# Banded attention: row sums taken from the exponentials and weights divided on GpSimd, in place of products with ones and a division at the end

## The chip, the cores and the metric

The kernel runs on one core of a Trainium2 chip. A core has five engines with queues of their own: TensorE (PE in the profile, with its weight loads as PEld), VectorE (DVE), ScalarE (ACT), GpSimd (POOL) and SyncE (SP, which here only issues DMAs). Each executes its instructions in the order in which they were put into its queue, and they wait for one another by semaphores.

The metric is the device time of one launch in microseconds. A run's time is a little longer than the span that its profile shows. Times are compared as medians over runs.

## The reference, cut to what matters

The reference is two transformer layers on an input of 16 sequences of 256 positions and 128 features, in float32. Layer 0 is full attention (16 heads of 64) and a feed-forward stage that picks one of 64 small networks for each position; layer 1 is a gated mix of linear and windowed attention, and then causal attention with eight experts behind it. Only the windowed attention of layer 1 is touched here:

```python
# WINDOW = 64, HALF = 32, NWIN = 65, N_HEADS = 16, HEAD_DIM = 8
def score_step(_, w):
    off = w - HALF
    ks = jax.lax.dynamic_slice_in_dim(kp, w, S, axis=2)
    s = jnp.einsum('bhsd,bhsd->bhs', qh, ks) * scale
    s = s + rel_bias[off + WINDOW][None, :, None]
    valid = (pos + off >= 0) & (pos + off < S)
    s = jnp.where(valid[None, None, :], s, -jnp.inf)
    return (None, s)
_, scores = jax.lax.scan(score_step, None, jnp.arange(NWIN))
attn = jax.nn.softmax(scores, axis=0)

def out_step(acc, aw):
    a, w = aw
    vs = jax.lax.dynamic_slice_in_dim(vp, w, S, axis=2)
    return (acc + a[..., None] * vs, None)
```

Each position looks at the 65 positions from 32 before to 32 behind it. The softmax is over these 65 scores, for each of 16 heads of 8 features.

## The kernel before

The 16 sequences are worked as 8 groups of 512 positions (two sequences each). A group passes through five stages: A (layer 0's attention), B (its feed-forward), C (layer 1's gated attention), D (causal attention) and E (the experts). Functions `stage_a` to `stage_e` do not issue instructions. They add tasks to a plan (`W.add`), each with the engine or the choice of engines ("VS" is DVE or ACT), a cost in ns, the tiles that it reads and writes, and a due time `at`: group g's stage A is due at g, B at g+1, and so on to E at g+4, so that up to five groups are in flight. `Plan.order` then walks through the tasks as a list scheduler. At each step it takes the task that can begin first by the costs, and of equals the one due first; it picks the engine where there is a choice and gives each buffer a slot from the pool of its class. The order that comes out is written into the engines' queues as it stands. A change of one cost, one task or one pool size (`SLOTS`) therefore gives another order for everything behind it.

Pools that the change touches: `x` (the groups' activations, 512 floats in each partition), `xT` (stage A's transposed input), `k1` (small tiles of stages B, C and E), `c` (the tiles of stage C), `pbC` (weights of the banded attention). `NX` is the number of groups whose input is loaded at the start; x of a later group is loaded by L291, into the slot of a group that was written out (L1331).

The banded attention stands in `stage_c`, from L1011. Each of a group's two sequences is cut into four blocks of 64 queries, 64 blocks in all. A block's keys are `nk` positions, 96 at the ends of the sequence and 128 inside. Two heads share the partitions of a tile: 64 queries of one and 64 of the next, so 16 heads make eight columns `u` of width nk.

1. GpSimd spreads the queries over the heads (`masked`, L1020), and DVE writes the values into one of three `vm` tiles so that head 4j+l stands in strip j with zeros beside it (L1036).
2. PE multiplies queries and keys (`scores`, L1046).
3. DVE adds the band of biases with -1e30 outside (L1053) and takes the negated maximum of each column (L1054).
4. For each of two halves, ACT takes four exponentials (L1065), PE transposes them (L1071), and DVE or ACT moves the result to SBUF (`ptC`; L520 is the helper's ACT form, L522 its DVE form).
5. PE multiplies with the values (`values`, L1078): for `what` 0 with `vm`, and for `what` 1 with `hones`, a tile of ones in the same strips. The second run of 16 products gives each query's sum of exponentials, repeated over the head's eight features.
6. DVE takes the reciprocal of the sums (L1098) and multiplies (L1099) into `winT`, which the gate at L1110 reads.

`mm` at L514 is the helper of every matrix product, so L514 stands for all of them in the profile; the tiles tell them apart. Stages A and D share the function `pair`: there ACT sums its exponentials as it takes them (L623, `accum_out`), DVE takes the reciprocals (L630), GpSimd divides (L636), and PE transposes (L651).

Of the kernel before, what the change touches and what calls it, by code (L numbers as in the profile page):

```python
# [30 lines left out]
NFC = FF // P  # L31
NEG = -1.0e30
EPS = 1e-5
NX = 6
NBURST = 2

OFF = {"a": 0.0, "b": 1.0, "c": 2.0, "d": 3.0, "e": 4.0}

SLOTS = (
    ("x", 512, 6),  # L40
    ("xT", 512, 2),
    ("ua", 512, 6),
    ("ud", 512, 6),
    ("pb", 512, 4),
    ("pt", 512, 4),
    ("ov", 256, 8),
    ("m", 64, 26),
    ("k1", 256, 5),
    ("b", 512, 2),
    ("sc", 288, 1),  # L50
    ("c", 512, 9),
    ("qm", 512, 2),
    ("pbC", 512, 2),
    ("ptC", 512, 2),
    ("d", 512, 3),
    ("h2", 512, 2),
# [181 lines left out]
def kernel(ctx: ExitStack, tc: tile.TileContext, a: dict, out: bass.AP):  # L238
# [8 lines left out]
    def ctile(name, shape, dtype=F32):  # L247
        return const.tile(shape, dtype, name=name, tag=name)
# [223 lines left out]
    nc.gpsimd.affine_select(  # L472
        out=hm, in_=hm, compare_op=ALU.is_ge, fill=0.0, base=WD - 1, pattern=[[WD, WH]], channel_multiplier=-1
    )

    hones = ctile("hones", [P, 4, 4 * WD])
    nc.gpsimd.memset(hones, 0.0)
    for l in range(4):
        nc.gpsimd.memset(hones[:, l, l * WD : (l + 1) * WD], 1.0)

    NVM = 3
    vms = []
# [30 lines left out]
    def mm(o, lhsT, rhs, start=True, stop=True):  # L513
        nc.tensor.matmul(o, lhsT=lhsT, rhs=rhs, start=start, stop=stop)  # L514
# [409 lines left out]
    def stage_c(g):  # L924
# [48 lines left out]
        for b in range(2):  # L973
            W.at = base + 0.1 + 0.4 * b

            pkv, kv = W.buf("p", "pkv"), W.buf("k1", "kv")

            def outer(b=b, pkv=pkv):
                for i in range(2):
                    k = kl(J, d=D)[:, 2 * b + i, :]  # L980
                    mm(pkv()[:, :D], k, vl(J, d=D)[:, 2 * b + i, :], start=i == 0, stop=i == 1)
                for i in range(2):
                    k = kl(J, d=D)[:, 2 * b + i, :]
                    mm(pkv()[:, D : D + 1], k, ones1, start=i == 0, stop=i == 1)

            W.add("P", pe(P, count=4), outer, r=[kl, vl], w=[pkv], hold=[kv])
            W.add("VS", (dve(129), scl(129)), lambda e, pkv=pkv, kv=kv: copy(e, kv()[:, : D + 1], pkv()[:, : D + 1]), r=[pkv], w=[kv])
            pn, rden = W.buf("p", "pn"), W.buf("m", "rden")

            def numer(b=b, pn=pn, kv=kv):  # L990
                for i in range(2):
                    j = 2 * b + i
                    mm(pn()[:, i * 256 : i * 256 + D + 1], ql()[:, j * P : (j + 1) * P], kv()[:, : D + 1])

            W.add("P", pe(P + 1, count=2), numer, r=[ql, kv], w=[pn], hold=[rden, lin])
            pn2 = lambda pn=pn: pn("p (i n) -> p i n", i=2)

            def divide(b=b, pn2=pn2, rden=rden):
                r = rden()[:, :2]
                V.tensor_scalar(r, pn2()[:, :, D], 1e-6, None, ALU.add)  # L1000
                V.reciprocal(r, r)
                V.tensor_tensor(
                    out=lin(J, d=D)[:, 2 * b : 2 * b + 2, :], in0=pn2()[:, :, :D],
                    in1=r.unsqueeze(2).to_broadcast([P, 2, D]), op=ALU.mult,
                )

            W.add("V", 360 + dve(256), divide, r=[pn], w=[rden, (lin, b)])

            for i, (w0, w1_) in enumerate(win_of):  # L1011
                W.at = base + 0.1 + 0.4 * b + 0.09 * i
                nk = w1_ - w0
                t0 = w0 - (QC * i - HALF)
                c0 = b * S + QC * i
                qm = W.buf("qm", "qm")
                nq = [P, WH // 2, QC]

                def masked(e, qm=qm, c0=c0, nq=nq):
                    (V if e == "V" else G).tensor_tensor(  # L1020
                        out=qm("p (h q) -> p h q", q=QC), in0=qw()[:, c0 : c0 + QC].unsqueeze(1).to_broadcast(nq),
                        in1=hm8.unsqueeze(2).to_broadcast(nq), op=ALU.mult,
                    )

                W.add("G", (gps(512),), lambda masked=masked: masked("G"), r=[qw], w=[qm])

                iv = nblock[0] % NVM
                nblock[0] += 1
                vm, vt = vms[iv], vmt[iv]
                pvw = W.buf("p", "pvw")  # L1030
                W.add("P", pe(P), lambda pvw=pvw, w0=w0, w1_=w1_, nk=nk, b=b: mm(pvw()[:nk, :D], hT()[:, b * S + w0 : b * S + w1_], wvw), r=[hT], w=[pvw, vt])

                def spread(pvw=pvw, vm=vm, nk=nk):
                    for l in range(4):
                        own = lambda t: t.rearrange("p (g e) -> p g e", e=4 * WD)[:, :, l * WD : (l + 1) * WD]
                        V.tensor_tensor(out=own(vm[:nk, l, :]), in0=own(pvw()[:nk, :D]), in1=own(bvw[:nk, :]), op=ALU.add)  # L1036

                W.add("V", 4 * dve(32), spread, r=[pvw], w=[vt])
                sps = W.buf("s", "spsC")

                def scores(sps=sps, qm=qm, w0=w0, w1_=w1_, nk=nk, b=b):
                    s4 = sps("p (t u k) -> p t u k", t=2, u=4)
                    for u in range(4):
                        for t in range(2):
                            r = slice(t * 64, (t + 1) * 64)
                            mm(s4[:, t, u, :nk], qm()[r, u * P : (u + 1) * P], kw()[r, b * S + w0 : b * S + w1_])  # L1046

                W.add("P", pe(nk, count=4), scores, r=[qm, kw], w=[sps, chain_c[0]], mode="r")
                nmx = W.buf("m", "nmxC")

                def top(sps=sps, nmx=nmx, nk=nk, t0=t0):
                    s8 = sps("p (u k) -> p u k", u=8)[:, :, :nk]
                    V.tensor_tensor(out=s8, in0=s8, in1=band[:, :, t0 : t0 + nk], op=ALU.add)  # L1053
                    V.tensor_reduce(nmx()[:, :8], s8, AX.X, ALU.max, negate=True)  # L1054

                W.add("V", 130 + 2 * dve(8 * nk), top, w=[sps, nmx])
                pts = []
                for half in range(2):
                    pb, pt, tps = W.buf("pbC", "pbC"), W.buf("ptC", "ptC"), W.buf("p", "tpsC")

                    def weigh(sps=sps, nmx=nmx, pb=pb, half=half, nk=nk):
                        s8 = sps("p (u k) -> p u k", u=8)
                        for u in range(4):
                            hp = 4 * half + u
                            act(pb("p (u k) -> p u k", u=4)[:, u, :nk], s8[:, hp, :nk], AF.Exp, bias=nmx()[:, hp : hp + 1])  # L1065

                    W.add("S", 4 * (146 + 0.81 * nk), weigh, r=[sps, nmx], w=[pb], table="exp")

                    def turn(pb=pb, tps=tps, nk=nk):
                        for u in range(4):  # L1070
                            nc.tensor.transpose(tps("p (u k) -> p u k", u=4)[:nk, u, :], pb("p (u k) -> p u k", u=4)[:, u, :nk], ident)  # L1071

                    W.add("P", pe(P, count=4, passes=1), turn, r=[pb], w=[tps, chain_c[1]], hold=[pt])
                    W.add("VS", (dve(512), scl(512)), lambda e, pt=pt, tps=tps, nk=nk: copy(e, pt()[:nk, :], tps()[:nk, :]), r=[tps], w=[pt])
                    pts.append(pt)
                po = W.buf("p", "poC")

                def values(po=po, pts=pts, vm=vm, nk=nk):  # L1078

                    for what in range(2):  # L1080
                        for l in range(4):
                            for j in range(4):
                                r = slice(32 * j, 32 * j + 32)
                                h = 4 * j + l
                                c = ((h // 2) % 4) * P + (h % 2) * QC
                                mm(
                                    po()[r, what * QC : (what + 1) * QC],
                                    hones[:nk, l, :] if what else vm[:nk, l, r],
                                    pts[j // 2]()[:nk, c : c + QC],
                                    start=l == 0,  # L1090
                                    stop=l == 3,
                                )

                W.add("P", 1200, values, r=[vt] + pts, w=[po, chain_c[2]], hold=[winT], mode="c32")
                rw = W.buf("m", "rw")

                def divide(po=po, rw=rw, c0=c0):
                    V.reciprocal(rw()[:, :QC], po()[:, QC : 2 * QC])  # L1098
                    V.tensor_tensor(out=winT()[:, c0 : c0 + QC], in0=po()[:, :QC], in1=rw()[:, :QC], op=ALU.mult)  # L1099

                W.add("V", 700, divide, r=[po], w=[rw, (winT, (b, i))])

        W.at = base + 0.95
        linT = W.buf("c", "linT")
# [273 lines left out]
```

## Time and profile before

| | |
|---|---|
| median of three runs | 2264.16 us (2259.54 to 2265.47) |
| time of the profiled run | 2259.16 us |
| its span in the profile | 2257.3 us, mean granted PE clock 0.98 |
| exponentials of the banded attention, L1065 | 512 |
| its transposes, L1071 | 512 |
| products with `vm`, records on PE | 2048, 43.2 us busy |
| DMA | 47.98 MB, 21 GB/s over the span |

A line of the groups of instructions reads: line, engine, operation, written tile <- read tiles, shapes, count | busy time in us, mean ns of one | idle time of the engine just before them, and what ended most of it. A float32 matrix product shows as two records. Tiles are named by their pool: `p` and `s` are PSUM, `m` holds small columns. A line of the list of waits reads: who waited, for whom, then us in sum, times, and the longest.

In the slices, a digit is the busy share of a fortieth of the span in tenths. Ends of matmuls are modelled, so the busy time of PE is a little more than what it holds the engine; the start of the next record is the safer mark. Spans on POOL are rough.

### The profile page before, as it was taken

To read this page: it belongs to the slowest core of one execution; us is meant where nothing else is said; L and a number is where in the kernel's file an instruction comes from. 1 tells how busy PE (TensorE), PEld (TensorE's weight loads), DVE (VectorE), ACT (ScalarE), POOL (GpSimd) and SP (SyncE) were. 2 spreads that over 40 slices of the span, in tenths; PEclk is the share of its full clock that TensorE was granted. 3 is DMA by queue.
4 is the path that set the end of the run, shared out by engine and by line. 5 is a ranking of instruction groups with operands and counts; after the bars stand their busy time and mean duration, and the time that the engine had idled before them with its cause. 6 is when DMAs were issued, how large, how long until landed. Compare 5 with 4: busy or idle time off the path is not lost.

```text
span 2257.3 us, 50085 instructions
## 1 busy us (share of the span) xinstructions
PE 2126.6 (94%) x18474; PEld 1611.8 (71%) x18474; DVE 1711.4 (76%) x5167; ACT 1316.0 (58%) x3824; POOL 801.7 (36%) x1441
## 2 busy tenths in 40 slices
PE   6999999999999999999999999999899989989987
PEld 5777767777777677776777767777667767767755
DVE  4789898888678977688767897588876976785741
ACT  3556656666466656565565666565565645654642
POOL 6435352444143531335213352143521441330421
PEclk8999999999999999999999999999999999999998
DMA  6100000000100001100010000100011001001101
GB/s 149 24 1 2 2 1 1 2 2 20 43 16 11 2 15 38 34 1 2 15 47 20 2 1 25 48 11 2 1 38 39 7 19 37 22 7 51 29 20 42
DMA packets 61029, 47.98 MB, mean 21 GB/s; under 512 B 4609, under 2 KB 51297, under 8 KB 60785
## 3 DMA queue, kind: packets, MB, share of 16 engines
q1 hardware_dynamic: 59200, 43.09, 6.8%
q8 instruction: 146, 2.39, 0.5%
q0 software_dynamic: 1008, 0.65, 0.3%
q10 hardware_dynamic: 576, 1.05, 0.2%
q14 instruction: 99, 0.80, 0.1%
HBM read 41.89 MB, written 2.88 MB: 20 GB/s over the span
## 4 chain that ended last, share of the span: by engine, by line
PE 31%; DVE 16%; ACT 3%; issue 2%; POOL 1%; POOLq 0%; DVEq 0%; ACTq 0%
PE p L514 25%; PE p L651 2%; PE s L514 2%; DVE m L602 2%; DVE s L597 1%; ACT pb L623 1%; DVE m L606 1%; DVE m L531 1%; POOL pb L636 1%; DVE s L1053 1%; DVE m L1054 1%; PE p L1071 1%; DVE m L1147 1%; DVE pt L522 1%; DVE m L1149 1%
## 5 line engine op out<-in xcount | busy, mean ns | idle before, releaser
L636 POOL TENSOR_SCALAR pb<-pb,m 128x256 f32<-128x256 f32 (+1 forms) x1024 | 452.4, 458 | 710.6 <-DVE m L630 611.2
L1309 ACT ACTIVATE hid<-p,b 128x512 f32<-128x512 f32 x256 | 169.3, 688 | 285.3 <-PE p L514 283.8
L651 PE MATMUL p<-ident,pb 128*128 128x128 f32 x1792 | 293.8, 284 | 22.4 <-POOL pb L636 17.0
L623 ACT ACTIVATE pb<-s,m 128x256 f32<-128x256 f32 x512 | 239.0, 488 | 112.5 <-DVE m L606 100.9
L623 ACT ACTIVATE pb<-s,m,m 128x128 f32<-128x128 f32 (+1 forms) x512 | 257.7, 525 | 62.3 <-DVE m L604 47.7
L651 PEld LDWEIGHTS p<-ident,pb 128*128 128x128 f32 x1792 | 208.1, 143 | 113.6 <-POOL pb L636 66.0
L514 PE MATMUL p<-h,we 128*128 128x512 f32 x512 | 251.5, 624 | 2.9 <-ACT hid L1309 2.5
L514 PEld LDWEIGHTS p<-we,hid 128*128 128x128 f32 x2048 | 238.6, 192 | 15.6 <-issue 10.0
L514 PE MATMUL p<-we,hid 128*128 128x128 f32 x2048 | 246.9, 276 | 1.0 <-ACT hid L1309 0.7
L520 ACT COPY pt<-p 128x384 f32<-128x384 f32 (+1 forms) x316 | 168.9, 541 | 122.6 <-PE p L651 115.7
L1217 POOL TENSOR_TENSOR kn<-kn,m 128x512 f32<-128x512 f32 x64 | 67.2, 1050 | 361.9 <-DVE m L630 224.0
L606 DVE TENSOR_REDUCE m<-s 128x4 f32<-128x1024 f32 x128 | 154.7, 1214 | 32.9 <-PE s L514 32.6
L514 PEld LDWEIGHTS p<-h,we 128*128 128x128 f32 x512 | 93.3, 197 | 98.9 <-issue 63.7
L1324 DVE SCALAR_TENSOR_TENSOR e<-p,m,e 128x128 f32<-128x128 f32 x256 | 71.7, 343 | 111.8 <-PE p L514 89.7
L514 PE MATMUL s<-ua,ua 64*128 64x256 f32 x1024 | 141.9, 401 | 10.9 <-ACT pb L623 10.8
L1065 ACT ACTIVATE pbC<-s,m 128x96 f32<-128x96 f32 (+1 forms) x512 | 135.1, 382 | 16.3 <-DVE m L1054 14.1
L514 PE MATMUL s<-ud,ud 64*128 64x128 f32 (+1 forms) x1024 | 115.7, 347 | 26.1 <-ACT pb L623 25.7
L522 DVE COPY pt<-p 128x512 f32<-128x512 f32 (+1 forms) x196 | 121.1, 623 | 22.1 <-PE p L651 19.9
L514 PE MATMUL p<-pt,ua 128*64 128x256 f32 x1024 | 136.8, 389 | 0.7 <-ACT pt L520 0.7
L602 DVE TENSOR_REDUCE m<-s 128x2 f32<-128x256 f32 (+1 forms) x256 | 130.8, 552 | 4.8
L514 PE MATMUL p<-pt,ud 128*64 128x256 f32 (+1 forms) x1024 | 117.7, 341 | 4.8 <-DVE pt L522 2.6
L514 PEld LDWEIGHTS s<-ua,ua 64*128 64x128 f32 x1024 | 92.0, 189 | 41.7 <-ACT pb L623 19.9
(298 smaller groups left out, 4420.3 us busy)
## 6 DMA issues: line engine op xcount, KB each, us to landing
we<-in_L_ffn_w_dram SPq DMA_DIRECT2D x128, 256.0 KB, 2.7
x<-_attn_hidden_states_dram SPq DMA_DIRECT2D x8, 256.0 KB, 5.3
out_dram<-x SPq DMA_DIRECT2D x8, 256.0 KB, 2.2
dpad<-k SPq DMA_DIRECT2D x1, 768.0 KB, 9.4
wq<-in_L_attn_Wq_dram ACTq DMA_DIRECT2D x2, 256.0 KB
wkv<-in_L_attn_Wkv_dram ACTq DMA_DIRECT2D x2, 256.0 KB, 7.3
wkv<-in_L_attn_Wkv_dram SPq DMA_DIRECT2D x2, 256.0 KB, 7.1
wo<-in_L_attn_Wo_dram SPq DMA_DIRECT2D x1, 512.0 KB, 11.2
```

The lines of the kernel that those rows point to most:

```text
L514: nc.tensor.matmul(o, lhsT=lhsT, rhs=rhs, start=start, stop=stop)
L520: nc.scalar.copy(o, i)
L522: nc.vector.tensor_copy(o, i)
L602: nc.vector.tensor_reduce(n[:, :, qc], s[:, :, c0 : c0 + nk], AX.X, ALU.max, negate=True)
L606: nc.vector.tensor_reduce(n, s.rearrange("p a (b k) -> p a b k", k=S), AX.X, ALU.max, negate=True)
L623: act(pb()[:, c0 : c0 + nk], s[:, par, c0 : c0 + nk], AF.Exp, bias=nmx()[:, 2 * par + qc : 2 * par + qc + 1], accum_out=sums()[:, 2 * par ...
L636: eng.tensor_scalar(pb()[:, c0 : c0 + nk], pb()[:, c0 : c0 + nk], sums()[:, 2 * par + qc : 2 * par + qc + 1], 1.0, ALU.mult, ALU.mult,)
L651: nc.tensor.transpose(tps()[:, at * P : (at + 1) * P], pb()[:, c0 + kc * P : c0 + (kc + 1) * P], ident)
L1065: act(pb("p (u k) -> p u k", u=4)[:, u, :nk], s8[:, hp, :nk], AF.Exp, bias=nmx()[:, hp : hp + 1])
L1217: lambda: G.tensor_tensor(out=kn("p (h d) -> p h d", d=DH), in0=kn("p (h d) -> p h d", d=DH), in1=rqk()[:, 8:16].unsqueeze(2).to_broadcast ...
L1309: W.add("S", 571, lambda ph=ph, hid=hid, ec=ec: act(hid(), ph(), AF.Gelu_apprx_tanh, bias=b1[:, ec : ec + 1]), r=[ph], w=[hid], table="gel ...
L1324: V.scalar_tensor_tensor(m, pe_()[:, j * D : (j + 1) * D], gate()[:, j * NE + e_ : j * NE + e_ + 1], m, ALU.mult, ALU.add)
```

## The change

Step 4 now also sums. The four exponentials of a half write their row sums to a small tile `smC` (`accum_out`), DVE takes the reciprocal of these four columns, and GpSimd multiplies the four columns of weights by it, in place in `pbC`, before PE transposes them. Step 5 loses the run with ones, and step 6 becomes one copy from PSUM to `winT`, on DVE or ACT as the plan decides. The tile `hones` and its memsets are gone. The costs given to the plan follow: 240 for 146 in each exponential's constant, 600 for 1200 in `values`.

Pool sizes change with it: `x` and `NX` from 6 to 5, `xT` 2 to 1, `k1` 5 to 4, `c` 9 to 8, `pbC` 2 to 3.

```diff
-NX = 6
+NX = 5
...
-    ("x", 512, 6),
-    ("xT", 512, 2),
+    ("x", 512, 5),
+    ("xT", 512, 1),
...
-    ("k1", 256, 5),
+    ("k1", 256, 4),
...
-    ("c", 512, 9),
+    ("c", 512, 8),
...
-    ("pbC", 512, 2),
+    ("pbC", 512, 3),
...
-    hones = ctile("hones", [P, 4, 4 * WD])
-    nc.gpsimd.memset(hones, 0.0)
-    for l in range(4):
-        nc.gpsimd.memset(hones[:, l, l * WD : (l + 1) * WD], 1.0)
...
-                            act(pb("p (u k) -> p u k", u=4)[:, u, :nk], s8[:, hp, :nk], AF.Exp, bias=nmx()[:, hp : hp + 1])
-
-                    W.add("S", 4 * (146 + 0.81 * nk), weigh, r=[sps, nmx], w=[pb], table="exp")
+                            act(pb("p (u k) -> p u k", u=4)[:, u, :nk], s8[:, hp, :nk], AF.Exp, bias=nmx()[:, hp : hp + 1],
+                                accum_out=sm()[:, u : u + 1])
+
+                    W.add("S", 4 * (240 + 0.81 * nk), weigh, r=[sps, nmx], w=[pb, sm], table="exp")
+                    W.add("V", 73, lambda sm=sm: V.reciprocal(sm()[:, :4], sm()[:, :4]), w=[sm])
+
+                    def share(pb=pb, sm=sm, nk=nk):
+                        w4 = pb("p (u k) -> p u k", u=4)[:, :, :nk]
+                        G.tensor_tensor(out=w4, in0=w4, in1=sm()[:, :4].unsqueeze(2).to_broadcast([P, 4, nk]), op=ALU.mult)
+
+                    W.add("G", gps(4 * nk), share, r=[sm], w=[pb])
...
-                    for what in range(2):
-                        for l in range(4):
-                            for j in range(4):
...
-                                mm(
-                                    po()[r, what * QC : (what + 1) * QC],
-                                    hones[:nk, l, :] if what else vm[:nk, l, r],
-                                    pts[j // 2]()[:nk, c : c + QC],
-                                    start=l == 0,
-                                    stop=l == 3,
-                                )
-
-                W.add("P", 1200, values, r=[vt] + pts, w=[po, chain_c[2]], hold=[winT], mode="c32")
-                rw = W.buf("m", "rw")
-
-                def divide(po=po, rw=rw, c0=c0):
-                    V.reciprocal(rw()[:, :QC], po()[:, QC : 2 * QC])
-                    V.tensor_tensor(out=winT()[:, c0 : c0 + QC], in0=po()[:, :QC], in1=rw()[:, :QC], op=ALU.mult)
-
-                W.add("V", 700, divide, r=[po], w=[rw, (winT, (b, i))])
+                    for l in range(4):
+                        for j in range(4):
...
+                            mm(po()[r, :QC], vm[:nk, l, r], pts[j // 2]()[:nk, c : c + QC], start=l == 0, stop=l == 3)
+
+                W.add("P", 600, values, r=[vt] + pts, w=[po, chain_c[2]], hold=[winT], mode="c32")
+                W.add(
+                    "VS", (dve(QC), scl(QC)),
+                    lambda e, po=po, c0=c0: copy(e, winT()[:, c0 : c0 + QC], po()[:, :QC]), r=[po], w=[(winT, (b, i))],
+                )
```

More of the change, by code (lines that the diff above doesn't have):

```diff
@@ L1058, in stage_c, with weigh @@
                 for half in range(2):
-                    pb, pt, tps = W.buf("pbC", "pbC"), W.buf("ptC", "ptC"), W.buf("p", "tpsC")
-                    def weigh(sps=sps, nmx=nmx, pb=pb, half=half, nk=nk):
+                    pb, pt, tps, sm = W.buf("pbC", "pbC"), W.buf("ptC", "ptC"), W.buf("p", "tpsC"), W.buf("m", "smC")
+                    def weigh(sps=sps, nmx=nmx, pb=pb, half=half, nk=nk, sm=sm):
                         s8 = sps("p (u k) -> p u k", u=8)
@@ L1078, in values @@
                 def values(po=po, pts=pts, vm=vm, nk=nk):
-                    for what in range(2):
-                        for l in range(4):
-                            for j in range(4):
-                                r = slice(32 * j, 32 * j + 32)
-                                h = 4 * j + l
-                                c = ((h // 2) % 4) * P + (h % 2) * QC
-                                mm(
-                                    po()[r, what * QC : (what + 1) * QC],
-                                    hones[:nk, l, :] if what else vm[:nk, l, r],
-                                    pts[j // 2]()[:nk, c : c + QC],
-                                    start=l == 0,
-                                    stop=l == 3,
-                                )
-                W.add("P", 1200, values, r=[vt] + pts, w=[po, chain_c[2]], hold=[winT], mode="c32")
-                rw = W.buf("m", "rw")
-                def divide(po=po, rw=rw, c0=c0):
-                    V.reciprocal(rw()[:, :QC], po()[:, QC : 2 * QC])
-                    V.tensor_tensor(out=winT()[:, c0 : c0 + QC], in0=po()[:, :QC], in1=rw()[:, :QC], op=ALU.mult)
-                W.add("V", 700, divide, r=[po], w=[rw, (winT, (b, i))])
+                    for l in range(4):
+                        for j in range(4):
+                            r = slice(32 * j, 32 * j + 32)
+                            h = 4 * j + l
+                            c = ((h // 2) % 4) * P + (h % 2) * QC
+                            mm(po()[r, :QC], vm[:nk, l, r], pts[j // 2]()[:nk, c : c + QC], start=l == 0, stop=l == 3)
[4 more added lines that the diff above has]
+                )
         W.at = base + 0.95
```

## The prediction

> **What bounds the kernel now.** I read the page's busy shares and 40-slice rows first.
>
> ```profile
> PE 2126.6 (94%) x18474; PEld 1611.8 (71%) x18474; DVE 1711.4 (76%) x5167; ACT 1316.0 (58%) x3824; POOL 801.7 (36%) x1441
> ...
> PE   6999999999999999999999999999899989989987
> ...
> PEclk8999999999999999999999999999999999999998
> ```
>
> PE is busy in nine tenths or more of nearly every slice, at full clock; it idles 2257.3 - 2126.6 = 131 us in all. The next engine, DVE, has a quarter of the span free. Work on PE is therefore the first suspect. I then cut the middle of the run into stretches of one group each (the chain of waits repeats every 271.2 us, so this is the period); one of them, as stretch, length, busy us with instruction counts, granted clock, DMA share, GB/s:
>
> ```profile
> 1096.40:1367.60 271.20, 261.29 (x2289) 197.48 (x2290) 210.76 (x631) 162.35 (x474) 94.34 (x170) 0.99 0.07 18
> ```
>
> Order: PE, PEld, DVE, ACT, POOL. Of 271.2 us PE is idle 10. So a group costs what its PE work costs, as long as the others keep feeding it. The list of waits says where they do not:
>
> ```profile
> PE s L514 <- ACT pb L623: 37.0, 29, 5.3
> PE p L651 <- POOL pb L636: 17.0, 9, 10.2
> ```
>
> These are the two longest sums, 54 of the 131 us; 10.2 us of the second is one wait in the start-up. The chain of waits also runs over DVE for 16% of the span against PE's 31%, so DVE is the engine that a stall would come from if its load grew.
>
> **What goes from PE.** The groups of instructions, shapes apart, have the products with ones:
>
> ```profile
> L514 PE MATMUL p<-ptC,hones 128*32 128x64 f32 x1024 | 20.5, 219 | 0.0
> L514 PE MATMUL p<-ptC,hones 96*32 96x64 f32 x1024 | 20.3, 219 | 0.0
> ```
>
> That is 40.8 us busy, but ends of matmuls overlap. The timeline of one block gives the pitch:
>
> ```profile
> 215.76 0.63 PE L514 MATMUL p<-ptC,hones 96*32 96x64 f32 x32
> ...
> 216.32 1.13 PE L514 MATMUL p<-wkv,xT 128*128 128x256 f32 x4
> ```
>
> The 32 records of a block (two for each of its 16 products) hold PE from 215.76 to 216.32, 0.56 us. There are 64 blocks (8 groups, 2 sequences, 4 windows): 64 x 0.564 = **36.1 us** off PE. No idle stands before these records (0.0 in both rows), so this is work and not a wait. In the built order of the changed kernel these 1024 products are the only matmuls missing from PE (10628 become 9604). If PE were covered by something else it would be worth nothing; at 10 idle us per 271.2 it is not covered.
>
> **What changes on DVE.** Gone are the reciprocal from PSUM and the product:
>
> ```profile
> L1098 DVE RECIPROCAL m<-p 128x64 f32<-128x64 f32 x64 | 35.1, 548 | 10.4 <-PE p L514 8.5 <-ACT pbC L1065 1.9
> ...
> L1099 DVE TENSOR_TENSOR c<-p,m 128x64 f32<-128x64 f32 x64 | 14.4, 224 | 2.2
> ```
>
> 49.5 us. Added: 128 reciprocals of 4 columns; the nearest row is L630's, 2 columns at 154 ns, so about 0.16 us each, 20.5 us. And 64 evacuations of 128x64 by copy, of which the built order puts about 34 on DVE and 30 on ACT; at L1099's 224 ns that is 7.6 us on DVE and about 7 on ACT. The order also moves other evacuations between the two: by counts times their rows, some 15 us more on DVE and as much less on ACT. DVE net: -49.5 + 20.5 + 7.6 + 15 = -6. It stays at 76%. The product L1099 also released PE late: its own view has PE waiting for it 1.6 + 1.0 us. A copy of one step instead of two takes that off: -2.6 us.
>
> **What changes on ACT.** 512 exponentials now sum as well. The price is not in this form in the trace. Without a sum, eight of them:
>
> ```profile
> 1125.20 1.96 ACT L1065 ACTIVATE pbC<-s,m 128x96 f32<-128x96 f32 x8 [0.97 <-DVE m L1054]
> ```
>
> (1.96 - 0.36) / 7 = 0.23 us apart. With a sum, 128x256, in stage A:
>
> ```profile
> 939.96 0.47 ACT L623 ACTIVATE pb<-s,m 128x256 f32<-128x256 f32 x1 [2.69 <-DVE m L606]
> 940.33 0.19 ACT L623 ACTIVATION_READ_ACCUMULATOR pb<-s,m 128x1 f32 x1
> 940.42 0.46 ACT L623 ACTIVATE pb<-s,m 128x256 f32<-128x256 f32 x1
> ```
>
> The reading starts 0.37 us after its exponential and the next exponential 0.09 after that, though its row says 0.19. Below: +0.09 us each, 48 us in all. Above: stage D's 128-wide form with a scale column follows itself after 0.44 us, against 0.25 for the 128-wide form without either: +0.19, 96 us. I take the lower end, since no scale column is added here. ACT goes from 1316 to some 1360 us (upper end 1410), 60%. Its own largest idle sum is 284 us before L1309, waiting for PE; that hides it. The path cost is the longer burst: 4 exponentials last 1.4 us and not 1.0, so the transposes of a half may come 0.4 us later; what that costs stands under the new wait.
>
> **What changes on POOL.** 128 products, half of them 128x512 in place by a broadcast column. L1217 is the same form:
>
> ```profile
> L1217 POOL TENSOR_TENSOR kn<-kn,m 128x512 f32<-128x512 f32 x64 | 67.2, 1050 | 361.9 <-DVE m L630 224.0 <-DVE m L1149 106.2 <-DVE m L1274 23.5
> ```
>
> 64 x 1.05 = 67 us; the 4x96 form lies between 0.79 (in proportion) and 1.05; at 0.84, 54 us. POOL goes from 802 to 923 us, 41%. [...] DVE's 128x512 product of two SBUF tiles, L970, takes 765 ns, so 1.37 times. [...] By the rows, 121 us go to an engine that sits idle 1455 us. I follow the rows. [...] The trace agrees that DVE pays:
>
> ```profile
> 930.80 1.11 DVE L544 TENSOR_SCALAR e<-e,m,m 128x128 f32<-128x128 f32 x4
> ...
> 946.06 1.38 DVE L544 TENSOR_SCALAR x<-e,m,m 128x128 f32<-128x128 f32 x4
> ```
>
> The first four ran with POOL idle, the second beside L636. The rows of L544 (362 to 497 ns against about 335 undisturbed), L604 and L1143 together show some 40 us of this, for 802 us of POOL: 0.05 us each. [...] by the trace 121 x 0.05 = 6 us. I take 6, inside DVE's free quarter.
>
> **The new wait.** A half's transposes waited for ACT; now they wait for ACT, then DVE, then POOL. Behind a late product on POOL stand stage A's and D's L636, for which PE waits. Behind a late transpose stands everything on PE. Bounds for 128 halves: below 0, since in the trace a half's transposes start a median of 2 to 3.6 us after its last exponential, with other PE work in between, and the longer burst and the new steps take 0.4 + 0.16 + 1.05 us and two hand-overs; above, one exposed product for each second half, 64 x 0.93 = 60 us. The nearest row is L651's wait above: without the start-up one, 6.8 us over 448 groups of transposes, 0.015 each, and 17.0 / 448 = 0.04 with it. I take 0.04: 128 x 0.04 = **+5 us**.
>
> **Smaller pools.** With 5 x buffers, x of group 5 loads after the output of group 0. On SyncE's timeline that output (L1331) is issued at 680.1 us, and the load behind it (L291, here of group 6) at 682.4; stage A of group 5 begins its projections at 771.3, so a load of 5.3 us to landing has over 80 us of room. If that room went, the delay would be what passes it. xT's second buffer is idle at the hand-over (old projections end at 743, new xT is written at 757). c, k1 and the third pbC I cost at nothing: in both built orders stage C of the next group starts behind the gate of the last, with as much PE work between. The ones' five memsets are 0.45 us of POOL.
>
> **Sum.** -36.1 - 2.6 + 5 = -33.7 us. Against the profiled run, 2259.16: 2225.5. The median of the three runs is 2264.16, which gives 2230.5; the profiled run lies at their lower edge. I base the forecast on the middle of the two, 2261.7: **2228**.
>
> **Rivals.**
> - The gain is half eaten: PE waits 0.15 us for each of 128 products (L651's weight loads wait 66 us for POOL over 448, 0.15 each): 2261.7 - 38.7 + 19 = 2242. For it: three engines in series. Against: the 2 to 3.6 us of room. 0.14.
> - Better than the sum: less idle PE, as DVE no longer holds blocks with a 548 ns reciprocal and the order is rebuilt. If 20 of 131 idle us go: 2261.7 - 38.7 - 20 = 2203. 0.14.
> - Slower: POOL's queue. the new product of each second half stands exposed, 60 us: 2261.7 - 38.7 + 60 = 2283. It decides from 38.7 / 128 = 0.30 us of PE wait per product, twice what PE's weight loads show. 0.07.
> - The work goes but the time does not: the period is held by another loop, such as stage C waiting for a c buffer, and the ones were hidden under it: 2262. Against: PE idles only 10 of 271.2. 0.06.
> - The forecast, 2216 to 2240: 0.59.
>
> Range 2202 to 2254: it leaves out the slower and the unchanged case, 0.13, and the far end of the better one. Three runs spread 0.26%, so 0.3% is what can be told from none. Faster 0.87, same 0.06, slower 0.07.
>
> **What would show it.** In the new profile: PE busy near 2090 us; no hones rows; about 131 us of idle PE; a period near 266 us; POOL near 923; L1065's readings at 0.09 us of pitch. I am wrong if PE waits for POOL pbC over 20 us, or if the idle time moves by more than 20.

## The result and the profile after

The changed kernel takes 2266.8 us (median of 20 runs, 2260.44 to 2272.87) against 2263.89 us for the kernel before (20 runs, 2258.59 to 2271.39). The ratio is 1.0012, with an interval from 1.0002 to 1.0023. Where 34 us less were forecast, the time stood still: about 3 us more.

The page of the changed kernel, busy time and share of each engine, the granted clock in fortieths of the span, and the chain of waits by engine:

```profile
PE 2112.8 (93%) x16426; PEld 1590.7 (70%) x16426; DVE 1713.5 (76%) x5228; ACT 1352.4 (60%) x4337; POOL 918.5 (41%) x1564
...
PEclk8999999999999999999999999999999999999998
...
PE 61%; DVE 27%; ACT 5%; POOL 3%; issue 3%; SPq 1%; DMA 1%; POOLq 0%; DVEq 0%; ACTq 0%
```

The loads on ACT and POOL are where the prediction had them (1360 and 923 us). PE is not: it lost 2048 records but only 13.8 us of busy time, where 36 were expected, and its span grew by 3.3 us. By the last line, more than a quarter of the way from start to end leads over DVE, although PE is busy 93% of the time. (The chain of the kernel before could be followed over about its second half only; there the two stood at 31 to 16, which is the same proportion.)

The lines of kernel.py have moved: in the changed kernel L509 is `mm` (L514 before), L618, L631 and L646 are the exponentials, the division and the transposes of stages A and D (L623, L636, L651), and of the banded attention L1060 are the exponentials, L1064 the reciprocals, L1068 the new product and L1074 the transposes.

Three things in the trace account for PE's 3.3 us. First, what the ones held. A block's products in the changed kernel, by the timeline of PE:

```profile
215.31 0.65 PE L509 MATMUL p<-ptC,vm 96*32 96x64 f32 x32
215.89 1.13 PE L509 MATMUL s<-ua,ua 64*128 64x256 f32 x8
```

From the first of these records to the next work are 0.58 us. Before, the values' run took 0.47 and the ones' run 0.56, together 1.03. The last run of a block is the longer one, whichever it is; the ones' departure saves 0.45 us of each block. Summed over the 64 blocks in the two traces it is 68.6 - 38.5 = 30.0 us and not 36.1.

Second, PE's idle time: the gaps between its records sum to 109.8 us before and 126.8 after, 17.0 more. The list of PE's waits after (who, for whom, us, times, longest):

```profile
PE p L646 <- POOL pb L631: 25.0, 20, 8.8
PE s L509 <- ACT pb L618: 21.6, 19, 2.9
PE p L1074 <- POOL pbC L1068: 14.4, 16, 2.6
PE s L509 <- ACT pbC L1060: 8.0, 9, 1.3
```

Third, the clock. The mean granted clock is 0.982 before and 0.977 after. The trace records stretches of half clock (0.50 granted), 3.41 us long or a multiple of it: 11 of them before the last instruction before, 18 after. PE is busy during most of them. Half of that busy time is counted here as lost, an estimate from the granted half: 26.1 us before, 39.9 after. So -30.0 + 17.0 + 13.8 = +0.8, and 2.5 us remain unexplained.

This is an account of two executions, not yet of causes, and its third term is not firm. The clock differs between runs of one kernel: over 89 runs of the kernel before it lies between 0.975 and 0.982, median 0.979, and the profiled one has the highest. The 20 runs of the changed kernel have a median of 0.976. The experiments ask which part of the change brings which share.

### The profile page after: what moved, and what is told of

Same layout as the page of the kernel before. It is cut to its first block, busy times and chain, and to the rows that moved or that the text cites. A ratio compares the mean times of both kernels' runs of the same rounds, so it can differ in the third digit from the quotient of the medians.

```text
span 2260.6 us, 46782 instructions
## 1 busy us (share of the span) xinstructions
PE 2112.8 (93%) x16426; PEld 1590.7 (70%) x16426; DVE 1713.5 (76%) x5228; ACT 1352.4 (60%) x4337; POOL 918.5 (41%) x1564
## 4 chain that ended last, share of the span: by engine, by line
PE 61%; DVE 27%; ACT 5%; POOL 3%; issue 3%; SPq 1%; DMA 1%; POOLq 0%; DVEq 0%; ACTq 0%
PE p L509 43%; PE s L509 8%; PE p L646 7%; DVE m L601 2%; DVE m L597 2%; PE p L1074 2%; POOL pb L631 1%; ACT pb L618 1%; DVE m L1049 1%; DVE s L1048 1%; DVE m L526 1%; DVE x L539 1%; DVE s L592 1%; ACT pbC L1060 1%; DVE m L1140 1%
## 5 line engine op out<-in xcount | busy, mean ns | idle before, releaser
L631 POOL TENSOR_SCALAR pb<-pb,m 128x256 f32<-128x256 f32 (+1 forms) x1024 | 451.9, 460 | 454.6 <-DVE m L625 351.4
L646 PE MATMUL p<-ident,pb 128*128 128x128 f32 x1792 | 293.9, 284 | 34.5 <-POOL pb L631 25.0
L618 ACT ACTIVATE pb<-s,m 128x256 f32<-128x256 f32 x512 | 238.6, 489 | 102.7 <-DVE m L601 89.1
L646 PEld LDWEIGHTS p<-ident,pb 128*128 128x128 f32 x1792 | 207.6, 143 | 120.2 <-POOL pb L631 71.0
L618 ACT ACTIVATE pb<-s,m,m 128x128 f32<-128x128 f32 (+1 forms) x512 | 259.4, 532 | 26.4 <-DVE m L599 21.5
L509 PEld LDWEIGHTS p<-we,hid 128*128 128x128 f32 x2048 | 241.9, 193 | 19.3 <-issue 11.4
L509 PE MATMUL p<-we,hid 128*128 128x128 f32 x2048 | 251.1, 278 | 1.7 <-ACT hid L1302 1.4
L509 PE MATMUL p<-h,we 128*128 128x512 f32 x512 | 243.7, 608 | 8.3 <-DVE m L1267 5.0
L515 ACT COPY pt<-p 128x384 f32<-128x384 f32 (+1 forms) x304 | 161.4, 540 | 127.0 <-PE p L646 103.1
L1060 ACT ACTIVATE pbC<-s,m 128x96 f32<-128x96 f32 (+1 forms) x512 | 175.2, 378 | 26.6 <-DVE m L1049 26.0
L1068 POOL TENSOR_TENSOR pbC<-pbC,m 128x384 f32<-128x384 f32 (+1 forms) x128 | 118.9, 935 | 161.6 <-DVE m L1064 114.0
L509 PEld LDWEIGHTS p<-h,we 128*128 128x128 f32 x512 | 91.7, 193 | 99.0 <-issue 61.5
L1015 POOL TENSOR_TENSOR qm<-c,hm 128x512 f32<-128x512 f32 x64 | 67.0, 1052 | 228.3 <-PE s L509 177.3
L509 PE MATMUL s<-ua,ua 64*128 64x256 f32 x1024 | 141.4, 401 | 13.3 <-ACT pb L618 9.1
L517 DVE COPY pt<-p 128x512 f32<-128x512 f32 (+1 forms) x208 | 129.1, 626 | 30.2 <-PE p L646 28.0
L509 PE MATMUL p<-pt,ua 128*64 128x256 f32 x1024 | 139.2, 391 | 3.4 <-DVE pt L517 1.0
L509 PE MATMUL s<-ud,ud 64*128 64x128 f32 (+1 forms) x1024 | 116.6, 348 | 17.0 <-ACT pb L618 11.7
```

The source lines that it names most:

```text
L515: nc.scalar.copy(o, i)
L517: nc.vector.tensor_copy(o, i)
L618: act(pb()[:, c0 : c0 + nk], s[:, par, c0 : c0 + nk], AF.Exp, bias=nmx()[:, 2 * par + qc : 2 * par + qc + 1], accum_out=sums()[:, 2 * par ...
L631: eng.tensor_scalar(pb()[:, c0 : c0 + nk], pb()[:, c0 : c0 + nk], sums()[:, 2 * par + qc : 2 * par + qc + 1], 1.0, ALU.mult, ALU.mult,)
L646: nc.tensor.transpose(tps()[:, at * P : (at + 1) * P], pb()[:, c0 + kc * P : c0 + (kc + 1) * P], ident)
L1068: G.tensor_tensor(out=w4, in0=w4, in1=sm()[:, :4].unsqueeze(2).to_broadcast([P, 4, nk]), op=ALU.mult)
```

## The experiments

All ratios are to the kernel before, run on the same chip in the same rounds. In a kernel whose order is kept, the plan is made as in its parent and only the issuing of some instructions is left out or altered. That matters here, since the plan rebuilds everything behind a changed task.

### The ones alone (e1)

```diff
-                    for what in range(2):
+                    for what in range(1):
...
-                    V.reciprocal(rw()[:, :QC], po()[:, QC : 2 * QC])
+                    V.reciprocal(rw()[:, :QC], po()[:, :QC])
```

> The kernel before with the products with ones left out and the order of everything else on all engines as it was (the division then divides the values by themselves, so the output is not the reference's). Theory W (the new wait on GpSimd and what follows from it gave the gain back): the work of the ones is on the path, its 64 x 0.47 us = 30 us go, 2234 us, ratio 0.987. Rival H (the ones were hidden anyway, something else holds the period): 2255 to 2264 us, ratio above 0.996.

Measured: 2259.46 us, ratio 0.9976 (0.9965 to 0.9988). This is what the rival forecast: 26.3 us left PE (68.6 to 42.3 us for these runs of products), and the time fell by some 5. Between the two traces PE's idle time grew by 10.5 us (109.8 to 120.2), and the loss to half clock by 12.2 (26.1 to 38.3). The second figure is not that of a usual run: in the same rounds the median clock was 0.978 before and 0.977 without ones, which is about 2 us of 2260. So what took the rest of the 26 us is shown in part only. Here is one place, four stretches of 3.4 us in the kernel without ones (busy us of PE, PEld, DVE, ACT, POOL with counts; then granted clock, DMA share, GB/s):

```profile
1312.80:1316.20 3.40, 2.81 (x16) 2.25 (x16) 3.33 (x5) 0.93 (x4) 2.26 (x2) 1.00 0.00 0
1316.20:1319.60 3.40, 1.77 (x15) 1.17 (x17) 3.40 (x22) 3.40 (x16) 2.15 (x5) 0.99 0.00 0
1319.60:1323.00 3.40, 3.40 (x17) 2.31 (x15) 2.90 (x7) 1.94 (x6) 3.14 (x7) 0.51 0.00 0
1323.00:1326.40 3.40, 3.15 (x29) 2.06 (x27) 3.17 (x11) 3.40 (x14) 2.16 (x6) 1.00 0.00 0
```

In the second stretch PE works 1.77 of 3.40 us while DVE and ACT work all of it. In the third PE gets half its clock. The timeline of the same place names the wait:

```profile
1317.41 0.93 PE L514 MATMUL s<-ud,ud 64*128 64x128 f32 x8 [1.80 <-ACT pb L623]
...
1319.23 1.83 PE L514 MATMUL s<-ua,ua 64*128 64x256 f32 x8 [0.42 <-ACT pb L623]
```

And the same place in the kernel before, by the timeline, and then the stretch with the wait and the next one, on the grid on which its clock changes:

```profile
1323.56 0.93 PE L514 MATMUL s<-ud,ud 64*128 64x128 f32 x8 [1.80 <-ACT pb L623]
...
1325.38 1.13 PE L514 MATMUL s<-ua,ua 64*128 64x256 f32 x8 [0.42 <-ACT pb L623]
...
1320.08:1323.50 3.42, 1.68 (x8) 1.14 (x6) 3.38 (x8) 2.08 (x9) 1.50 (x2) 1.00 0.00 0
1323.50:1326.91 3.41, 2.93 (x22) 1.83 (x22) 3.38 (x19) 3.17 (x12) 3.02 (x8) 1.00 0.00 0
```

The waits for ACT, 1.80 and 0.42 us, are the same to the hundredth; with less work on PE they were no shorter. (In the list of waits they even grow in sum, from 37.0 us to 41.7.) In the kernel without ones the eight products behind them run at half clock and take 1.83 us and not 1.13. Before, PE was busy no longer in the stretch with the wait, 1.68 us, and still had its full clock in the next; why the one was slowed and not the other is not shown.

### The division alone, and both together (e14, e13)

e14 keeps the ones, order and all, and replaces reciprocal and product by one copy; e13 does so without the ones.

```diff
-                    V.reciprocal(rw()[:, :QC], po()[:, QC : 2 * QC])
-                    V.tensor_tensor(out=winT()[:, c0 : c0 + QC], in0=po()[:, :QC], in1=rw()[:, :QC], op=ALU.mult)
+                    V.tensor_copy(winT()[:, c0 : c0 + QC], po()[:, :QC])
```

> The kernel before, order kept and the products with ones kept, with one copy in place of reciprocal and product at the end (the output is undivided). It prices the division alone, 64 x 0.55 us of VectorE. If it was on the path: 2245 to 2255 us. If it was hidden: 2260 us or more.

Measured: 2249.18 us, 0.9933 (0.9910 to 0.9956). The division was on the path.

> The kernel before, order kept, without the products with ones and with one copy in place of reciprocal and product at the end (the weights stay undivided): the operations of e3 in the old order. If the division on VectorE was what held the old order: about 2240 us, as e3. If the new order is what is better: 2252 to 2259 us, as e1.

Measured: 2247.48 us, 0.9925 (0.9900 to 0.9950), between its two forecasts. In both kernels DVE's busy time falls from 1711.4 us to 1680, by 31 us, and e14 shows 15 of them in the time. With that gone, taking 26 us from PE as well gives another 2, within the error. So in this order the work of the engine that is busy 76% weighed more than that of the one that is busy 94%. Whether by its load on DVE or by the 0.55 us that it stands in a block's own chain, e14 cannot tell.

### The new order, without the new operations (e3, e2)

e2 is the changed kernel without the product on GpSimd (first pair of lines); e3 also lacks the sums and their reciprocals.

```diff
-                        G.tensor_tensor(out=w4, in0=w4, in1=sm()[:, :4].unsqueeze(2).to_broadcast([P, 4, nk]), op=ALU.mult)
+                        pass
...
-                            act(pb("p (u k) -> p u k", u=4)[:, u, :nk], s8[:, hp, :nk], AF.Exp, bias=nmx()[:, hp : hp + 1],
-                                accum_out=sm()[:, u : u + 1])
+                            act(pb("p (u k) -> p u k", u=4)[:, u, :nk], s8[:, hp, :nk], AF.Exp, bias=nmx()[:, hp : hp + 1])
...
-                    W.add("V", 73, lambda sm=sm: V.reciprocal(sm()[:, :4], sm()[:, :4]), w=[sm])
+                    W.add("V", 73, lambda sm=sm: None, w=[sm])
```

> The changed kernel without the division of the weights on GpSimd; order, pools and plan as in the changed kernel (the weights stay undivided). Theory W: PE's waits for POOL fall from 46 us to about 15, and half-clock time with them: 2228 to 2240 us, ratio to before 0.984 to 0.990. Rival O (the rebuilt order and the smaller pools cost it, whatever GpSimd does): 2255 us or more, ratio above 0.996.

Measured: 2251.37 us, 0.9942 (0.9928 to 0.9956), between the forecasts of W and O. PE's waits for POOL fell to 28.5 us and not to 15, and the loss to half clock did not fall (40.8 us), so theory W's account is not borne out.

> As the last, and also without the sums in the exponentials and the reciprocals of these sums. Theory W: at most 5 us less than the last run, 2225 to 2238 us. Rival S (the longer bursts on ACT give the gain back): 15 us or more less than the last run. Rival O: as the last run, 2255 us or more.

Measured: 2238.17 us, 0.9883 (0.9866 to 0.9901). So both operations cost: the product 1.0012 - 0.9942 = 0.0070, 16 us; the sums with their reciprocals 0.0059, 13 us. Rival S, which was to show 15 us or more, is nearer than theory W with its 5. The 13 us are not ScalarE's alone, since the reciprocals take 10 us of VectorE with them (1698.9 to 1688.5 us). e3 also runs 0.0042, some 9 us, below e13, which has the same kinds of work in the old order; the intervals of the two touch.

### The sums in the old order (e11)

```diff
-                            act(pb("p (u k) -> p u k", u=4)[:, u, :nk], s8[:, hp, :nk], AF.Exp, bias=nmx()[:, hp : hp + 1])
+                            act(pb("p (u k) -> p u k", u=4)[:, u, :nk], s8[:, hp, :nk], AF.Exp, bias=nmx()[:, hp : hp + 1],
+                                accum_out=spare[:, 4 * half + u : 4 * half + u + 1])
```

> The kernel before with its order kept, where the exponentials of the banded attention also sum (into a tile that nobody reads). Theory S (the longer bursts on ACT cost time in any order, as the 13 us in the changed order suggest): 2272 to 2280 us. Rival (ACT has room, the 13 us were of that order): 2262 to 2268 us.

Measured: 2295.88 us, 1.0135 (1.0122 to 1.0148), beyond both. The price on ACT is what was estimated. The changed kernel's timeline of ACT:

```profile
359.18 0.36 ACT L1060 ACTIVATE pbC<-s,m 128x128 f32<-128x128 f32 x1
359.43 0.20 ACT L1060 ACTIVATION_READ_ACCUMULATOR pbC<-s,m 128x1 f32 x1
359.52 0.37 ACT L1060 ACTIVATE pbC<-s,m 128x128 f32<-128x128 f32 x1
```

The reading starts 0.25 us after its exponential, when the next exponential used to start, and that one follows 0.093 later (median); 512 x 0.093 = 48 us, and in e11 ACT's busy time rises by 45. But 31 us show in the time, on an engine that is idle 42% of it. In the order of the changed kernel, which was planned with the longer bursts, the sums and their reciprocals together cost 13 us.

### Where the product costs (e5, e9)

e5 writes the product to a tile that nobody reads, so that nothing waits for it.

```diff
-                        G.tensor_tensor(out=w4, in0=w4, in1=sm()[:, :4].unsqueeze(2).to_broadcast([P, 4, nk]), op=ALU.mult)
+                        G.tensor_tensor(out=waste.rearrange("p (u k) -> p u k", u=4)[:, :, :nk], in0=w4, in1=sm()[:, :4].unsqueeze(2).to_broadcast([P, 4, nk]), op=ALU.mult)
```

> The changed kernel with its order kept and its GpSimd products still made, but written to a tile that nobody reads; the transposes take the undivided weights and so wait for ACT alone. Theory W1 (of the 15 us that the product costs, most is PE waiting for the product itself): 2250 to 2255 us, as without the product. Theory W2 (most is what the product does to others, by GpSimd's queue and by VectorE operations that slow down beside it): 2262 to 2267 us, as the changed kernel.

Measured: 2265.48 us, 1.0008 (0.9998 to 1.0018), as the changed kernel. The wait of 14.4 us that the list shows for the product costs nothing: without it PE waits as long for something else (its idle time is 128.6 us; the wait for the exponentials of the banded attention, 8.0 us in the changed kernel, is 15.2). The 16 us lie in what the product does to others. VectorE is one candidate. Two of stage D's small operations in the changed kernel, by groups of instructions:

```profile
L1134 DVE TENSOR_SCALAR m<-m 128x16 f32<-128x16 f32 x64 | 18.2, 284 | 1.3
...
L1136 DVE TENSOR_SCALAR m<-m 128x16 int32<-128x16 int32 x64 | 17.3, 270 | 2.5
```

The same two without the product (e2), same view:

```profile
L1134 DVE TENSOR_SCALAR m<-m 128x16 f32<-128x16 f32 x64 | 14.5, 227 | 1.2
L1136 DVE TENSOR_SCALAR m<-m 128x16 int32<-128x16 int32 x64 | 14.5, 227 | 2.4
```

Of these 128 operations in the changed kernel, the 66 with no GpSimd operation beside them took at most 175 ns; those beside one took up to 1203. The longest began just after a GpSimd operation (here an older one, L911) and ended with it:

```profile
2151.46 1.26 POOL L911 TENSOR_TENSOR e<-e,lngb 128x512 f32<-128x512 f32 x1
2151.55 1.20 DVE L1136 TENSOR_SCALAR m<-m 128x16 int32<-128x16 int32 x1
```

VectorE's busy time is 1713.5 us with the product and 1698.9 without, 14.6 us, where 6 were estimated. e9 then cut each product into four short ones:

```diff
-                        G.tensor_tensor(out=w4, in0=w4, in1=sm()[:, :4].unsqueeze(2).to_broadcast([P, 4, nk]), op=ALU.mult)
+                        for u in range(4):
+                            G.tensor_scalar(w4[:, u, :], w4[:, u, :], sm()[:, u : u + 1], 1.0, ALU.mult, ALU.mult)
```

> The changed kernel with its order kept and each product on GpSimd issued as four short ones of one head column (the form of the line that divides the weights of stages A and D, 0.38 us for 128 wide) in place of one of 1.04 or 0.83 us. GpSimd works longer, about 50 us in all, but never more than 0.4 us at a stretch. Theory L (the product costs because small VectorE operations stand still until a running GpSimd operation ends): VectorE's busy time falls by 5 us or more and the time to 2250 to 2260 us. Theory Q (it costs because GpSimd's own queue runs later): 2270 us or more.

Measured: 2264.88 us, 0.9997 (0.9988 to 1.0006). VectorE falls by 6.8 us, as theory L has it, while GpSimd grows by 55; the time falls by about 3 us, hardly more than the error. Neither range was hit. That VectorE is busy longer with the product is shown (14.6 us); how the 16 us divide between VectorE's longer operations and GpSimd's own queue running later stays open.

### PE's work put back (e10)

The changed kernel with its order, and the 1024 products with ones behind those of the values, their result unread (`hones` and its memsets come back with them).

```diff
+                    for l in range(4):
+                        for j in range(4):
...
+                            mm(po()[r, QC : 2 * QC], hones[:nk, l, :], pts[j // 2]()[:nk, c : c + QC], start=l == 0, stop=l == 3)
```

> The changed kernel with its order kept and the 1024 products with ones put back behind the values' products; nobody reads their result. Theory H2 (PE's time is half shared with waits and half-clock windows, so 26 to 30 us of PE work weigh less than half): 2270 to 2280 us, with fewer half-clock windows and less idle time than in the changed kernel. Theory W (PE's work is on the path one for one): 2293 to 2300 us.

Measured: 2285.11 us, 1.0080 (1.0068 to 1.0092), 15 us above the changed kernel for 28.6 us more in these runs. It lies between the two forecasts. Idle time fell by 5 us (126.8 to 122.1), but the loss to half clock did not (42.5 us), so that part of H2 is wrong. In this order PE's work is worth about half of its length, against a fifth in the old one (e1).

### Order and pools (e6, e4, e12, e7, e8, e15)

e6 has exactly the work of the kernel before. The plan is told two measured costs, and with the order it also chooses anew which engine makes some of the copies:

```diff
-                W.add("P", 1200, values, r=[vt] + pts, w=[po, chain_c[2]], hold=[winT], mode="c32")
+                W.add("P", 1031, values, r=[vt] + pts, w=[po, chain_c[2]], hold=[winT], mode="c32")
...
-                W.add("V", 700, divide, r=[po], w=[rw, (winT, (b, i))])
+                W.add("V", 772, divide, r=[po], w=[rw, (winT, (b, i))])
```

> The kernel before with the same instructions in another order: the plan is told 1031 and 772 ns, the measured costs, for the values' products and the division, in place of 1200 and 700. It measures how much another order alone moves the time. If order is worth little: 2258 to 2270 us. If a new order is worth as much as the parts of the change: more than 10 us away from 2264 on either side.

Measured: 2278.52 us, 1.0073 (1.0055 to 1.0091). Better costs gave a slower kernel: 16 us, as much as any single part of the change. VectorE is busy 18 us less in it (1693.3 us) and ScalarE 13 more, so VectorE's load does not set the time by itself.

e4 and e12 put pools back, e4 all of them, e12 all but `xT` and `pbC` (the lines marked here are e4's; e12 has the first, second, fourth and fifth):

```diff
-NX = 5
+NX = 6
-    ("x", 512, 5),
+    ("x", 512, 6),
-    ("xT", 512, 1),
+    ("xT", 512, 2),
-    ("k1", 256, 4),
+    ("k1", 256, 5),
-    ("c", 512, 8),
+    ("c", 512, 9),
-    ("pbC", 512, 3),
+    ("pbC", 512, 2),
```

> The changed kernel with all pools as before (x 6, xT 2, k1 5, c 9, pbC 2). Theory W: 2255 to 2275 us, as the changed kernel, since the wait on GpSimd stays. Rival O in its form with the pools: 2230 to 2245 us.

> The changed kernel with x 6, k1 5 and c 9 as before, xT 1 and pbC 3 as changed; the order is rebuilt. If the smaller pools cost: 2250 us or less. If they are harmless and only another order comes out: anywhere within 20 us of 2267.

Measured: e4 2284.5 us, 1.0085 (1.0068 to 1.0103); e12 2263.6 us, 0.9994 (0.9983 to 1.0004). e4 is outside both of its forecasts. With the larger `x`, `k1` and `c` alone (e12) the time is 4 us lower, in an order of its own; since another order is worth more than that, this is not a price of the pools. e4's 21 us above e12 come with the larger `xT`, one `pbC` less and another order, which it cannot tell apart.

e7 adds 600 ns to the product's cost in the plan; e8 lets the plan choose GpSimd or VectorE for it (`share` then issues it on the engine chosen):

```diff
-                    W.add("G", gps(4 * nk), share, r=[sm], w=[pb])
+                    W.add("G", gps(4 * nk) + 600, share, r=[sm], w=[pb])
...
+                    W.add("GV", (gps(4 * nk), dve(4 * nk)), share, r=[sm], w=[pb])
```

> The changed kernel with 600 ns added to the product's cost in the plan alone, so that the order leaves more room between a product and its transposes. Theory W1: PE's waits for the products fall from 14 us to under 6, 2250 to 2260 us. Theory W2: 2260 to 2272 us.

> The changed kernel with the product on GpSimd or VectorE as the plan decides; 64 of 128 go to VectorE. If GpSimd is what gives the gain back: 2250 to 2260 us. If VectorE has as little room: 2262 to 2275 us.

Measured: e7 2292.46 us, 1.0141 (1.0120 to 1.0161); e8 2325.24 us, 1.0276 (1.0256 to 1.0296). Both missed, on the slow side. Half the products on VectorE make it 28 us busier (1741.8 us), and idle PE time rises to 161.5 us, but each of these two also has a new order, so the sizes are not those of the edit alone.

e15, the four short products with e12's pools, was the try at a version that beats both:

> The changed kernel with the four short GpSimd products of e9 and the pools of e12 (x 6, k1 5, c 9). If the two small gains add: 2257 to 2262 us, below both kernels. If not: 2263 to 2268 us.

Measured: 2267.12 us, 1.0008 (0.9993 to 1.0022). It doesn't. No complete version ran below the kernel before beyond doubt.

### The bill

Steps between these kernels, as differences of ratios times 2264 us; by the intervals of the ratios each is known to some 4 to 8 us:

| step | us |
|---|---|
| division to copy, ones kept (e14) | -15 |
| ones, the division gone (e13 from e14) | -2 |
| new order and pools, some copies on another engine (e3 from e13) | -9 |
| sums and their reciprocals (e2 from e3) | +13 |
| product on GpSimd (changed from e2) | +16 |
| sum | +3 |

This is one way through the parts, and their prices depend on the way. The ones are worth 2 us behind the division, 5 alone in the old order (e1) and 15 in the new one (e10). By e10 everything else of the change costs 18 us, and the ones give 15 back.

## Why the prediction was wrong

**"This is work and not a wait ... it is not covered."** This is the step that failed. From PE's 94% and its 10 idle us in 271 the prediction took every microsecond on PE for one of the time. e1 gave about 5 us for 26, and e10, in the new order, 15 for 28.6. In the place shown the waits of PE for ACT stayed as long as they were (1.80 and 0.42 us); PE only reached them earlier. The remark that the chain ran over DVE for half as long as over PE stood in the same paragraph and was read as a warning about more load on DVE, not as a price for less.

**"+5" for all that was added.** This step failed as well, and by about as much. The sums with their reciprocals and the product cost 13 + 16 = 29 us. Without them (e3) the time was 2238 us, close to the forecast of 2228. But at most 15 of those 26 us came from the ones, where the sum had 36, and the rest from the division and the order, where it had 2.6: had the added parts been free, the number would have come out by luck. The prediction's two signs of being wrong did not appear, since PE's wait for the product, 14.4 us, and its idle time, 17 us more, stayed under 20.

**"64 x 0.564 = 36.1 us."** Mis-sized: 30.0 in the changed kernel's trace. The last run of a block takes 0.56 to 0.58 us and one before another 0.47, whichever products they are.

**DVE net -6, -2.6 for the late product.** The sum was right (1711 to 1713 us). The path effect of the division was not: 64 x 0.55 us gave 15 us (e14), not 2.6.

**ACT "hides it".** The price of a sum was right at 0.09 us. The cover was not there: 31 us in the old order, and 13 with the reciprocals in the new one. The 284 us of ACT's idle time before L1309 are waits in stage E's bursts; the runs do not show how much of them lay beside the banded attention.

**GpSimd and VectorE, 6 us "inside DVE's free quarter".** VectorE lost 14.6 us (1713.5 with the product, 1698.9 without). The price was not in the speed of the product: GpSimd's rows came out as read (1040 and 830 ns). The small VectorE operations are nearer to it: in the changed kernel those of L1134 and L1136 took at most 175 ns with no GpSimd operation beside them and up to 1203 beside one, though e9 leaves open how much of the 16 us this is.

**The new wait, +5.** The list after has 14.4 us of it, and taking it away gave nothing (e5). The step asked the right engine the wrong question: not who waits for the product, but who is late beside it.

**Smaller pools, nothing.** Not contradicted for `x`, `k1` and `c` (4 us, e12, in another order); `xT` and `pbC` were not tried alone.

**The clock** was read as full and left out of the sum. It is not a constant: among runs of the kernel before alone it goes with 12 us of the time (last section).

**The order** was costed at nothing as well: the prediction compared where the stages begin and not what a new order is worth. It is worth about 9 us here in the change's favour (hardly beyond the error), and 16 against in e6.

Of the rivals, "the work goes but the time does not", at 0.06, had the outcome; for its mechanism, a wait for a buffer of stage C, the runs show nothing (with a ninth `c` buffer, e12, the gain does not appear).

## What to carry to other kernels

Where engines run fixed queues against one another, as here, the busy share need not tell the bound (26 us off PE at 94% gave 5, 31 off VectorE at 76% gave 15): price an edit by leaving out that one piece with the order kept, on the engine suspected and on the next one. Idle time elsewhere in the span was no cover: ScalarE was idle 42% of it and 48 us of added work still cost 31. Where a scheduler rebuilds the order, measure first what another order with the same work does; a gain below that cannot be credited to the edit.

## What the runs showed of the hardware

In the traces half clock followed long idle time of PE. The granted clock changed between 1.00 and 0.50 on a grid of 3.41 us. Counted up to PE's last work, all 7 full-clock stretches of this grid with PE busy under 40% were followed by half clock in the kernel before, and of the 620 followed by full clock none was under 46%. (From 391.67 us on, for instance, PE was busy 1.15 of 3.41 us, and the stretch behind had 0.50.) In the changed kernel it was 9 of 9, and none of 608 was under 50%. So in both, each full-clock stretch with over 2.05 us of idle PE had half clock behind it. Idle time is not all of it: in the kernel before 4 more stretches followed by half clock had PE busy 52 to 87%, and the two shown under e1 with about half (1.77 of 3.40 us and 1.68 of 3.42) went different ways. In all 17 traces together 140 of 140 stretches under 40% were followed by half clock, and 149 others were, too. What sets the clock is not shown.

The clock also goes with most of the spread between runs of one kernel. The 18 runs of the kernel before at a granted 0.982 took 2259.5 us in the median, its 6 at 0.975 took 2271.3, with the others in order between. So two single runs differed by 12 us without any change of the kernel, and a difference in clock between kernels is to be read from the medians. No run held the clock and changed the idle time alone.

The 128 VectorE operations of L1134 and L1136 on 16 columns took 174 ns in the median with no GpSimd operation beside them and up to 1203 ns with one beside them. With the 128 new GpSimd operations, 119 us in all, VectorE was busy 14.6 us longer (1713.5 us against 1698.9 in e2), 0.12 us for each microsecond of GpSimd. With each cut into four short ones it was busy 6.8 us less (e9).
